# A depthwise convolution inside an attention kernel: from whole 128-token chunks with half of the TensorE array per head to half chunks with a quarter of the array per head, added up from two PSUM banks

## The chip, the cores and the metric

The kernel runs on one core of one Trainium2 chip. The metric is device time in microseconds for one execution of the whole program; the median of three runs is used.

## The reference

There are two layers on a feature map of 2 batches, 512 channels and 64 x 32 = 2048 tokens. All numbers are fp32.

Layer 0 is a full softmax attention with 8 heads of 64 channels. Layer 1 is a Nystrom attention: with 256 landmarks per head it forms three softmax matrices, takes a pseudo-inverse of the middle one in 6 iterations, and adds to the attention's result a convolution of the values along the tokens:

```python
attn2_pinv = moore_penrose_iter_pinv(attn2, PINV_ITERS)
out = attn1 @ (attn2_pinv @ (attn3 @ v))
pad = KERNEL // 2
res = lax.conv_general_dilated(v, conv_w, window_strides=(1, 1), padding=((pad, pad), (0, 0)),
                               dimension_numbers=('NCHW', 'OIHW', 'NCHW'), feature_group_count=h)
out = out + res
```

`KERNEL` is 33. Every head has one filter of 33 taps, which runs over the head's 2048 tokens in each of its 64 channels. An output projection, a normalisation and a linear map (4-bit weights times a second matrix) follow. The change concerns only `res`.

## The kernel before

The kernel works on **pairs of heads**: 2 batches x 4 pairs make 8 pairs, and 2 heads x 64 channels fill the 128 partitions. Layer 0 takes the first part of the program (up to about 1620 us), then come the projections of layer 1 for all pairs, and from about 1800 us on the pairs of layer 1 are worked through one after the other in the order of `todo` (batch 1 first, then batch 0). The main loop (`for n, pair in enumerate(todo)`) runs `pair.pinv(chunk, last)`. The pseudo-inverse of pair n is a chain of dependent matmuls, and between its steps the callbacks `chunk` and `last` put work of the neighbouring pairs: `attn1` of pair n-1 (`before`), `attn3`, the convolution and the landmarks of pair n+1 (`after`), the value projection of pair n+2, and at n >= 4 the output stage of batch 1 (`finish`).

The order of the instructions of PE, DVE, ACT and POOL is the order in which the code writes them (`tc.manual_schedule(engines=in_order)`). The queue of SP, which starts most DMAs, is ordered by the scheduler.

The **convolution** of pair n+1 stands in `chunk(NTB)`, after the last full iteration of the pseudo-inverse: `landmarks = after.landmarks_values(); next(landmarks); drain(convolution(n + 1))`. Only the first pair is different: `second_of_first` puts its convolution in two parts among the projections (1728.5 and 1738.8 us). The convolution is done as a matmul with a band matrix. `write_bands` writes for every head a row with the 33 taps into DRAM in such a way that, read back with a row length that is one shorter, each partition's copy is shifted by one; `prefetch` loads the band of a pair (tile `band`, one buffer). `convolution` (line 1433 is its matmul) goes over 4 blocks t of 512 tokens. For each it takes one PSUM bank `cv`, lets every chunk of 128 tokens that reaches into the block add 160 columns (128 plus 16 on either side) in each head's half of the bank's partitions, and ACT copies the bank out (line 1442, or 1445 followed by a DMA to `o_fd`). The chunks overlap by 32 columns, so the matmuls of a block accumulate.

Four further facts are needed to follow the steps:

- PSUM in this part has four banks in one pool (tag `pp`), two for products of the pseudo-inverse and two side banks. `bank(...)` takes one of the four, which go round in the order in which they come free; `cv`, the row sums `rs` of `landmarks_values` (line 1380), the transposes `tp_M` of `flip` (line 1496) and `wp` of `product_transposed` (line 1481) all come from the four.
- Ahead of the convolution `chunk(NTB)` writes the end of the last `attn1` block of pair n-1: `attn1_inverse` (line 1595, DVE reciprocal) and `attn1_end` (line 1600, DVE product, then POOL adds into `o`). At n = 5 and 6 a step of `finish` is next (lines 957, 958 and 962, DVE). Then `landmarks_values` writes an ACT copy (line 1389), a DVE reciprocal (line 1390) and a DVE product (line 1391). All of these stand ahead of the convolution in the queue of DVE.
- After the convolution `pinv` goes on with `flip` for both heads (PE transposes `tp_M`, ACT copies M, line 1497), and with `product_transposed`, whose second half of matmuls needs the flipped M. Then comes the value projection `vp` (line 924) of pair n+2.
- For `todo[5]` and `todo[6]` `o` is None: the rows go through a two-buffer tile (`row_of`, tag `rinv`) and by DMA to `o_fd`, so the third row waits for the first row's DMA. The last pair has a buffer of its own again.

Of the kernel before, what the change touches and what calls it, by code (L numbers as in the profile page):

```python
# [10 lines left out]
F32 = mybir.dt.float32  # L11
I32 = mybir.dt.int32
AF = mybir.ActivationFunctionType
ALU = mybir.AluOpType
AX = mybir.AxisListType

P = 128
# [3 lines left out]
HEADS, D = 8, 64  # L21
NPAIR = HEADS // 2
TB = 512
NTB = S // TB
NST = S // P
LM, POOL = 256, S // 256
PINV_ITERS = 6
KER, HALO = 33, 16
# [624 lines left out]

CUBE = 0.25 ** (1.0 / 3.0)

BAND = P + 2 * HALO

GAP = object()

# [2 lines left out]
def fast_path(  # L662
# [35 lines left out]
    nc = tc.nc  # L698
    dram = ctx.enter_context(tc.tile_pool(name="dram1", bufs=1, space=bass.MemoryType.DRAM))
# [20 lines left out]
    o_d = dram.tile([B, NPAIR, P, S], F32, name="o_fd")  # L720
    A_d = dram.tile([B, NPAIR, 2, P, 2, LM], F32, name="A_fd")
    L_d = dram.tile([B, NPAIR, P, 2, LM], F32, name="L_fd")
    band_d = dram.tile([HEADS, P * (BAND + 1)], F32, name="band_fd")

    def chunked(ap):
        return ap.rearrange("(k p) n -> p k n", p=P)
# [1 line left out]
    def bank(name):  # L728
        return ps.tile([P, 512], F32, tag="pp", name=name)
# [21 lines left out]
    def block_of(pool, tag, name):  # L751
        return pool.tile([P, KC, TB], F32, tag=tag, name=name)

    def row_of(name):
        return apool.tile([P, TB], F32, tag="rinv", name=name)
# [417 lines left out]
    def write_bands():  # L1173


        rows = block_of(lpool, "xn", "rows1").rearrange("p k n -> p (k n)")
        rows = rows[:, : HEADS * (BAND + 1)].rearrange("p (h q) -> p h q", h=HEADS)
        nc.vector.memset(rows, 0.0)
        nc.sync.dma_start(rows[:, :, :KER], convr.partition_broadcast(P))
        for h in range(HEADS):  # L1180
            nc.sync.dma_start(band_d[h].rearrange("(p q) -> p q", q=BAND + 1), rows[:, h, :])

    class Pair:
# [120 lines left out]
        def prefetch(self):  # L1304
            self.k = kvpool.tile([P, S], F32, tag="v", name=f"k2_{self.name}")
            nc.sync.dma_start(self.k, k_d[self.b, self.hp])
            self.L = [lmpool.tile([P, LM], F32, tag="L0", name=f"L0_2_{self.name}")]
            nc.sync.dma_start(self.L[0], L_d[self.b, self.hp][:, 0, :])
            self.band = lmpool.tile([P, 2, BAND], F32, tag="band", name=f"band_{self.name}", bufs=1)
            for h in range(2):  # L1310
                src = band_d[2 * self.hp + h][: P * BAND].rearrange("(p q) -> p q", q=BAND)
                nc.sync.dma_start(self.band[:, h, :], src)

        def values(self, xhs):
            v = kvpool.tile([P, NST, P], F32, tag="v", name=f"v_{self.name}")
# [104 lines left out]

        def convolution(self, o):

            self.o = o
            for t in range(NTB):
                toks = slice(t * TB, (t + 1) * TB)
                cv = bank(f"cv_{self.name}_{t}")
                near = [c for c in range(4 * t - 1, 4 * t + 5) if 0 <= c < NST]
                for c in near:
                    at = c * P - HALO - t * TB
                    lo, hi = max(0, -at), min(BAND, TB - at)  # L1430
                    for h in range(2):
                        half = slice(h * D, (h + 1) * D)
                        nc.tensor.matmul(  # L1433
                            cv[half, at + lo : at + hi],
                            lhsT=self.v[:, c, half],
                            rhs=self.band[:, h, lo:hi],
                            start=c == near[0],
                            stop=c == near[-1],
                            skip_group_check=True,
                        )  # L1440
                if o is not None:
                    nc.scalar.copy(o[:, toks], cv)
                else:
                    row = row_of(f"o_{self.name}_{t}")
                    nc.scalar.copy(row, cv)
                    nc.sync.dma_start(o_d[self.b, self.hp][:, toks], row)
                if t % 2:
                    yield

# [228 lines left out]
    for n, (b, hp) in enumerate(todo[:-1]):  # L1678
        nb, nhp = todo[n + 1]
        if nb != b:  # L1680
            xbs = load_x(x, nb, "x0")
        nxt = Heads0(nb, nhp, xbs)
        n_fill = Heads0.N_UNITS + 2 * len(work)
        if finish is None:
            units = nxt.units(wait=nb - b)
        else:

            units = nxt.units(False, lambda: outs_done)
            work.append(finish)
            n_fill += N_FINISH0  # L1690
        work.append(units)
        attention0(cur, work, n_fill, units, ffn_map if finish is None else None, finish is not None)
        finish = None
        oTs.append(cur.q)
        if n == 3:
            while ffn_map:
                advance(ffn_map)
            wo_sb = load_wo(wo0, "wo_f0")
            write_bands()
        if hp == NPAIR - 1:  # L1700
            outs_done = []
            finish = finish0_units(b, oTs, outs_done)
            oTs = []
        cur = nxt
# [126 lines left out]
    def second_of_first():  # L1831
        pair = todo[0]
        yield from values(0)
        yield from pair.attn3()
        landmarks, start, conv = pair.landmarks_values(), pair.start_values(), convolution(0)
        for part in (landmarks, conv, landmarks, start, conv):
            next(part)
            yield
        drain(conv)
        next(start)  # L1840
        yield
# [26 lines left out]
    for n, pair in enumerate(todo):  # L1868
# [16 lines left out]
        if n:  # L1885
            q = late_buffer if n > NPAIR + 1 else lambda name: kvpool.tile([P, S], F32, tag="k", name=name)
            pair.prefetch1(q(f"q2_{pair.name}"))

        def chunk(c):
# [5 lines left out]
            if c == NTB:  # L1895
                if after:
                    landmarks = after.landmarks_values()
                    next(landmarks)
                    drain(convolution(n + 1))
                else:  # L1900
                    advance(finish, 2)
                return
# [126 lines left out]
@with_exitstack  # L2029
def conv_attn_hybrid(  # L2030
    ctx: ExitStack,
    tc: tile.TileContext,
    x: bass.AP,
    emb: bass.AP,
    freq: bass.AP,
    time: bass.AP,
    wq0: bass.AP,
    wk0: bass.AP,
    wv0: bass.AP,
    wo0: bass.AP,  # L2040
    b0: bass.AP,
    *rest: bass.AP,
):

    nc = tc.nc
    keep = ctx.enter_context(tc.tile_pool(name="keep_f", bufs=1))
    bad = keep.tile([P, 1], F32, name="bad")
    bad_i = keep.tile([P, 1], I32, name="bad_i")
    in_order = {mybir.EngineType.PE, mybir.EngineType.DVE, mybir.EngineType.Activation, mybir.EngineType.Pool}
    with tc.manual_schedule(engines=in_order):  # L2050
        fast_path(tc, x, freq, time, wq0, wk0, wv0, wo0, b0, *rest, bad)
    nc.vector.tensor_copy(bad_i, bad)
    again = nc.values_load(bad_i[:1, :1])
    with tc.If(again > 0):
        general_path(tc, x, emb, wq0, wk0, wv0, wo0, b0, *rest)
# [59 lines left out]
```

## Time and profile before

| | |
|---|---|
| median of 3 runs | 2808.86 us (2808.78 to 2810.7) |
| profiled execution, its own time | 2808.29 us |
| profiled execution, span from first to last instruction | 2806.2 us |
| granted TensorE clock, mean | 0.993 |
| busy: PE / PE weight loads / DVE / ACT / POOL | 98% / 49% / 63% / 33% / 8% |
| convolution on PE (line 1433) | 704 matmuls, 40.3 us |

A line of the groups names the line of code, the engine, the operation and the tiles, then the busy time in us and the mean ns of one instruction, then the idle time just before and what ended it. In "128*64 128x160" the first part is the piece of the array that is used (rows*columns), the second the moving operand. One fp32 matmul of the code appears as two MATMUL records with a weight load (LDWEIGHTS) each, called passes below: 352 matmuls of the convolution are 704 records. Matmuls of several pieces of the array that stand next to each other run side by side, so the busy time divided by the count is smaller than the duration of one.

### The profile page before, as it was taken

Reading aid. Unit: us, or ns where it says so; the run is one execution under the profiler, and the core shown is the slowest. Engines: PE = TensorE matmul, PEld = TensorE weight load, DVE = VectorE, ACT = ScalarE, POOL = GpSimd, SP = SyncE. Lnnn points to the kernel's source line nnn. Section 1 sums busy time; section 2 is a strip of 40 time slices with the busy share of each in tenths; the row PEclk is TensorE's granted clock in tenths of the full one; section 3 lists DMA queues with packets and bytes.
Section 4 is the critical chain, followed back from the end, with each engine's and each line's share of the span. In section 5 each row is a group of like instructions: output and inputs, shape, how many; then the busy total and the mean of one; then the engine's idle time right before and its main releaser. Section 6 shows DMA issues by size and latency. Waiting matters only on the chain. (4 is left out here: it accounts for less than half of the span.)

```text
span 2806.2 us, 39647 instructions
## 1 busy us (share of the span) xinstructions
PE 2745.0 (98%) x16746; PEld 1374.3 (49%) x16746; DVE 1778.3 (63%) x2109; ACT 913.5 (33%) x1352; POOL 231.7 (8%) x130
## 2 busy tenths in 40 slices
PE   9999999999999999999999999999999999999899
PEld 5343443434343334343344455777667666554333
DVE  2868788784658775767767544545755655556565
ACT  1434343433334334434422223223332323222110
POOL 1101101010101210100002000000100100000000
PEclk9999999999999999999999999999999999999999
DMA  3000000101001200002025632203001102010201
GB/s 113 5 5 1 5 1 1 61 16 46 27 32 60 75 1 1 1 31 67 16 83 180 202 120 89 97 28 114 27 28 50 65 1 86 23 61 19 101 16 46
DMA packets 85626, 140.31 MB, mean 50 GB/s; under 512 B 7856, under 2 KB 42944, under 8 KB 82880
## 3 DMA queue, kind: packets, MB, share of 16 engines
q1 hardware_dynamic: 80944, 120.87, 12.8%
q0 software_dynamic: 4416, 16.79, 1.6%
q8 instruction: 133, 2.18, 0.3%
q14 instruction: 53, 0.43, 0.0%
q10 hardware_dynamic: 80, 0.03, 0.0%
HBM read 82.48 MB, written 55.19 MB: 49 GB/s over the span
## 5 line engine op out<-in xcount | busy, mean ns | idle before, releaser
L1058 DVE TENSOR_TENSOR acc_f<-acc_f,p_f 128x1024 f32<-128x1024 f32 x448 | 611.4, 1365 | 217.8 <-ACT p_f L1048 188.8
L1048 ACT ACTIVATE p_f<-sc_f 128x1024 f32<-128x1024 f32 x512 | 496.8, 1022 | 580.2 <-PE sc_f L1040 574.1
L1040 PE MATMUL sc_f<-q_f,k_f 64*64 64x512 f32 x4096 | 491.7, 595 | 2.9 <-ACT p_f L1048 2.9
L1070 PE MATMUL av_f<-p_f,v_f 64*64 64x512 f32 x4096 | 484.3, 589 | 0.0
L1070 PEld LDWEIGHTS av_f<-p_f,v_f 64*64 64x64 f32 x4096 | 156.5, 133 | 283.0 <-issue 283.0
L1040 PEld LDWEIGHTS sc_f<-q_f,k_f 64*64 64x64 f32 x4096 | 144.8, 133 | 293.8 <-issue 253.0
L1214 PE MATMUL pp<-xh,w 128*128 128x512 f32 x512 | 231.2, 604 | 4.6 <-ACT X L1261 3.9
L1214 PEld LDWEIGHTS pp<-xh,w 128*128 128x128 f32 x512 | 95.7, 192 | 125.8 <-issue 113.9
L1506 PE MATMUL pb<-R 128*128 128x192 f32 (+1 forms) x640 | 149.6, 380 | 1.0 <-DVE M L1519 1.0
L1506 PE MATMUL pa<-M 128*128 128x192 f32 (+1 forms) x640 | 150.6, 380 | 0.0
L1595 DVE RECIPROCAL acc<-acc 128x256 f32<-128x256 f32 x64 | 111.4, 1746 | 46.7 <-ACT acc L1590 46.7
L1089 POOL TENSOR_TENSOR q_f<-q_f,rinv_f 128x512 f32<-128x512 f32 x32 | 68.3, 2135 | 825.6 <-DVE rinv_f L1088 825.5
L1601 POOL TENSOR_TENSOR o<-o,acc 128x512 f32<-128x512 f32 x32 | 53.8, 1682 | 885.1 <-DVE acc L1600 778.1
L924 PE MATMUL vp<-w,xh 128*128 128x128 f32 x1024 | 122.3, 278 | 0.0
L924 PEld LDWEIGHTS vp<-w,xh 128*128 128x128 f32 x1024 | 118.6, 194 | 7.2 <-issue 4.2
L924 PEld LDWEIGHTS vp_f<-wv_f,x 128*128 128x128 f32 x1024 | 115.6, 192 | 12.7 <-issue 11.0
L879 PE MATMUL pp_q_f<-x,wq_f 128*128 128x512 f32 x256 | 117.5, 612 | 4.2 <-DVE q_f L882 3.1
L939 PE MATMUL yp_f<-q_f,wo_f 128*128 128x512 f32 x256 | 115.9, 606 | 4.2 <-DVE rinv_f L1088 3.3
L924 PE MATMUL vp_f<-wv_f,x 128*128 128x128 f32 x1024 | 118.5, 276 | 0.0
L1506 PEld LDWEIGHTS pb<-R 128*128 128x128 f32 x640 | 106.5, 190 | 24.4 <-DVE M L1519 2.1
L1506 PEld LDWEIGHTS pa<-M 128*128 128x128 f32 x640 | 108.2, 193 | 20.4 <-ACT M L1497 2.5
L1654 PE MATMUL fp_g<-xn_g,mT 128*128 128x512 f32 x256 | 115.1, 598 | 0.7 <-ACT p L1568 0.7
(202 smaller groups left out, 3009.6 us busy)
## 6 DMA issues: line engine op xcount, KB each, us to landing
xh<-xh_fd SPq DMA_DIRECT2D x12, 1024.0 KB, 5.4
xr_f<-in_x_dram SPq DMA_DIRECT2D x8, 1024.0 KB, 5.1
x_fd<-xr_f POOLq DMA_DIRECT2D x8, 1024.0 KB, 4.7
xh_fd<-xn_f POOLq DMA_DIRECT2D x8, 1024.0 KB, 4.6
k_fd<-k SPq DMA_DIRECT2D x32, 256.0 KB, 2.7
q_fd<-q SPq DMA_DIRECT2D x32, 256.0 KB, 3.0
xb_g<-x_fd SPq DMA_DIRECT2D x32, 256.0 KB, 4.5
k<-k_fd SPq DMA_DIRECT2D x8, 1024.0 KB, 5.9
```

Source lines behind the costliest of these rows:

```text
L879: nc.tensor.matmul(pp, lhsT=w_sb[kind][:, k, cols], rhs=xbs[t][:, k, :], start=k == 0, stop=k == KC - 1)
L924: nc.tensor.matmul(vp[:, j * P : (j + 1) * P], lhsT=xb[:, k, j * P : (j + 1) * P], rhs=w_of(k), start=k == 0, stop=k == KC - 1,)
L939: nc.tensor.matmul(yp, lhsT=wo_sb[:, k, m * P : (m + 1) * P], rhs=oTs[k][:, toks], start=k == 0, stop=k == NPAIR - 1,)
L1040: nc.tensor.matmul(sc[r * D : (r + 1) * D, h, :], lhsT=hd.k[rows, lo : lo + D], rhs=hd.q[rows, t * TB : (t + 1) * TB], start=True, stop=True,)
L1048: nc.scalar.activation(p, sc, AF.Exp, scale=D**-0.5)
L1058: nc.vector.tensor_tensor(acc, first if c == 1 else acc, p, ALU.add)
L1070: nc.tensor.matmul(av[r][half, :], lhsT=hd.v[keys, c, half], rhs=pp[keys, h, :], start=c == 0, stop=c == NST - 1,)
L1089: nc.gpsimd.tensor_tensor(o, o, rinv, ALU.mult)
L1214: nc.tensor.matmul(pp, lhsT=self.w[j][:, c, :], rhs=xhs[t][:, c, :], start=c == 0, stop=c == KC - 1)
L1506: nc.tensor.matmul(dst, lhsT=lhsT[:, k, t * P : (t + 1) * P], rhs=rhs[:, k, :], start=k == 0, stop=k == 1)
L1595: nc.vector.reciprocal(half, half)
L1654: nc.tensor.matmul(fp, lhsT=mT[:, k, m * P : (m + 1) * P], rhs=self.xn[:, k, :], start=k == 0, stop=k == KC - 1,)
```

## The change

The 128-token chunk is split into two halves of 64 tokens (r = 0, 1), which are the lower and the upper 64 partitions of `v`. A half chunk reaches 16 tokens further on either side, 96 columns in all; the band row is laid out so that each matmul writes 128 columns, the 96 and 32 in which the band is zero. Even halves write columns that lie side by side without overlap or gap, and so do odd halves. The even ones go to one bank, the odd ones to another (`cvs[0]`, `cvs[1]`), each matmul with `start=True, stop=True`. A head's half chunk uses 64 rows and 64 columns of the array. ACT copies one bank to the destination, and DVE adds the other bank onto it in place; at the ends of the sequence, where one of the banks isn't filled in full, it is the one that is added, with 480 columns. The band is loaded into both halves of the partitions, with four DMAs in place of two.

```diff
-BAND = P + 2 * HALO
+BAND = P
...
-    band_d = dram.tile([HEADS, P * (BAND + 1)], F32, name="band_fd")
+    band_d = dram.tile([HEADS, D * (BAND + 1)], F32, name="band_fd")
...
-        rows = rows[:, : HEADS * (BAND + 1)].rearrange("p (h q) -> p h q", h=HEADS)
+        rows = rows[:D, : HEADS * (BAND + 1)].rearrange("p (h q) -> p h q", h=HEADS)
         nc.vector.memset(rows, 0.0)
-        nc.sync.dma_start(rows[:, :, :KER], convr.partition_broadcast(P))
+        nc.sync.dma_start(rows[:, :, HALO : HALO + KER], convr.partition_broadcast(D))
...
-                src = band_d[2 * self.hp + h][: P * BAND].rearrange("(p q) -> p q", q=BAND)
-                nc.sync.dma_start(self.band[:, h, :], src)
+                src = band_d[2 * self.hp + h][: D * BAND].rearrange("(p q) -> p q", q=BAND)
+                for r in range(2):
+                    nc.sync.dma_start(self.band[r * D : (r + 1) * D, h, :], src)
...
-                cv = bank(f"cv_{self.name}_{t}")
-                near = [c for c in range(4 * t - 1, 4 * t + 5) if 0 <= c < NST]
-                for c in near:
-                    at = c * P - HALO - t * TB
-                    lo, hi = max(0, -at), min(BAND, TB - at)
-                    for h in range(2):
-                        half = slice(h * D, (h + 1) * D)
-                        nc.tensor.matmul(
-                            cv[half, at + lo : at + hi],
-                            lhsT=self.v[:, c, half],
-                            rhs=self.band[:, h, lo:hi],
-                            start=c == near[0],
-                            stop=c == near[-1],
-                            skip_group_check=True,
-                        )
-                if o is not None:
-                    nc.scalar.copy(o[:, toks], cv)
-                else:
-                    row = row_of(f"o_{self.name}_{t}")
-                    nc.scalar.copy(row, cv)
-                    nc.sync.dma_start(o_d[self.b, self.hp][:, toks], row)
+                cvs = [bank(f"cv{r}_{self.name}_{t}") for r in range(2)]
+                for c in range(max(4 * t - 1, 0), min(4 * t + 5, NST)):
+                    for r in range(2):
+                        at = c * P + r * D - 2 * HALO - t * TB
+                        lo, hi = max(0, -at), min(BAND, TB - at)
+                        if lo >= hi:
+                            continue
+                        rows = slice(r * D, (r + 1) * D)
+                        for h in range(2):
+                            half = slice(h * D, (h + 1) * D)
+                            nc.tensor.matmul(
+                                cvs[r][half, at + lo : at + hi],
+                                lhsT=self.v[rows, c, half],
+                                rhs=self.band[rows, h, lo:hi],
+                                start=True,
+                                stop=True,
+                            )
+                dst = o[:, toks] if o is not None else row_of(f"o_{self.name}_{t}")
+
+                full, part, cols = cvs[0], cvs[1], slice(2 * HALO if t == 0 else 0, TB)
+                if t == NTB - 1:
+                    full, part, cols = cvs[1], cvs[0], slice(0, TB - 2 * HALO)
+                nc.scalar.copy(dst, full)
+                nc.vector.tensor_tensor(dst[:, cols], part[:, cols], dst[:, cols], ALU.add)
+                if o is None:
+                    nc.sync.dma_start(o_d[self.b, self.hp][:, toks], dst)
```

## Prediction

> **What bounds the kernel now.** I read the page's shares of the span, then the groups, then the timeline of one convolution, engine by engine. The page and its groups:
>
> ```profile
> PE 2745.0 (98%) x16746; PEld 1374.3 (49%) x16746; DVE 1778.3 (63%) x2109; ACT 913.5 (33%) x1352; POOL 231.7 (8%) x130
> ...
> L1433 PE MATMUL cv<-band,v 128*64 128x144 f32 (+2 forms) x704 | 40.3, 270 | 0.0
> L1077 DVE TENSOR_TENSOR q_f<-av_f,q_f 128x512 f32<-128x512 f32 x32 | 22.0, 689 | 8.0 <-ACT q_f L1076 8.0
> L1442 ACT COPY o<-cv 128x512 f32<-128x512 f32 x24 | 14.1, 587 | 16.4 <-PE cv L1433 16.4
> ```
>
> PE is busy 98% of the span and the convolution's matmuls never wait (idle 0.0), so every us that the convolution takes or waits on PE is a us of the program, unless PE waits for the same thing later anyway. ACT waits for PE, not PE for ACT. The other two lines are prices. Now one of the seven convolutions in the main loop (the one that starts at 2030.28), first DVE's timeline, then PE's (start, length, engine, line):
>
> ```profile
> 2030.14 1.75 DVE L1595 RECIPROCAL acc<-acc 128x256 f32<-128x256 f32 x1
> 2031.93 0.69 DVE L1600 TENSOR_TENSOR acc<-av,acc 128x512 f32<-128x512 f32 x1
> 2032.54 1.74 DVE L1390 RECIPROCAL acc<-acc 128x256 f32<-128x256 f32 x1
> 2034.38 0.42 DVE L1391 TENSOR_TENSOR acc<-av,acc 128x256 f32<-128x256 f32 x1
> 2040.98 0.48 DVE L1519 SCALAR_TENSOR_TENSOR R<-M,tp 128x128 f32<-128x128 f32 x2 [6.17 <-PE tp L1490]
> ```
>
> ```profile
> 2030.28 5.00 PE L1433 MATMUL cv<-band,v 128*64 128x144 f32 x88
> 2035.22 0.44 PE L1496 MATMUL tp_M<-ident,M 128*128 128x128 f32 x2
> 2035.58 1.37 PE L1481 MATMUL wp<-M 128*64 128x256 f32 x8
> 2036.88 3.84 PE L924 MATMUL vp<-w,xh 128*128 128x128 f32 x32
> ```
>
> DVE's share of 63% hides what matters: at just this place DVE has a queue of four instructions that ends at 2034.80, 4.52 us after the convolution began and 0.4 us before PE leaves it. Today nothing of the convolution is behind them. From here all times are counted from a convolution's first matmul: PE reaches tp_M at 4.93, wp at 5.30, vp at 6.60.
>
> [...]the trace has four copies of 587 ns per convolution whatever PE does. [...]at 1003.00, from 64*64 to 128*128, the trace shows a gap of 0.09 us. [...]above, DVE runs its four in the written order. [...]the eight 16-column matmuls from 1729.62 on start 25.4 ns apart on average, the densest 64 of the trace 50.8 ns.
>
> **The change part by part.**
>
> *PE, the passes.* From the single records: two 160-column matmuls side by side take 136 ns per pass, 144 columns 122 ns, 16 columns 59 ns[...]. So 128 columns take about 109 ns. In layer 0 four 64*64 matmuls of 512 columns start 7 ns apart and take 429 ns per pass, with their weight loads side by side, so I let four quarters of 128 columns take 109 ns as well. A block t becomes 4 steps of 128 columns and one at the seam, 2 passes each: 8 x 109 + 2 x 59 = 0.99 us. Today blocks follow each other after 1.27 us (the ACT copies start at 2031.61, 2032.87, 2034.14). Four blocks: 3.96 against 4.93 us, **0.97 less per convolution**, 7.8 us in eight, if nothing waits. Matmul records go from 704 to 1216 (76 matmuls per pair in place of 44). One more change of mode per convolution, 0.1 us, stays in the rounding.
>
> *DVE, the adds.* 32 instructions like line 1077, 0.69 us for 512 columns and 0.65 for 480, starting 0.6 us apart when they follow each other (the pace at which neighbours start above): 22 us on an engine with spare time. But in DVE's order they stand behind line 1391. If f is the time when 1391 ends, add 0 ends at f+0.58 and add 1 at f+1.20 (each starts up to 0.07 early).
>
> *Banks.* A block takes two of the four, and one of them is freed by the add. In the built program's order and waits, six of the seven loop convolutions have it so: block 2 needs the ACT copies of 0 and 1; **block 3 waits for add 0 and then add 1**; tp_M of head 1 waits for add 2; wp waits for the ACT copy of block 3. Queued behind the waiting matmul is all of PE. At n = 0 it is block 2 that waits for add 0, and block 3 for add 1.
>
> *Where PE comes out.* With f = 4.52: block 3 starts in earnest at f+1.26 = 5.78 and PE is through 0.87 later; ACT sees it 0.17 later and copies for 0.59; wp starts 0.06 after (7.47) in place of 5.30. Its first half takes 0.55, by which time both flips are in (today PE waits for them), its second 0.57: vp at 8.6 in place of 6.60, **2.0 later** (f+4.07). Three convolutions are of this kind (1931.5, 2030.3, 2129.1): 6.0 us. The others:
> - 1832.7 (no attn1 ahead): f = 2.93, block 2 starts at 3.57, block 3 ends at 5.45, vp at 7.4: +0.8.
> - 2227.8 (rows to DRAM): the third ACT copy waits for the first row's DMA, which now leaves after add 0. Today it lands 2.30 after the row is written (1.91 to 4.21). Row 0 at 5.10, copies of blocks 2 and 3 at 7.4 and 8.0, add 2 done at 8.74, then tp_M, flip, second half of wp: vp at 10.07 in place of 7.03: +3.0.
> - 2340.8 (rows, and lines 957/958 ahead): f = 7.34, row 0 at 7.92, by the same steps vp at 12.9 in place of 7.10: +5.8.
> - 2479.5 (line 962 ahead): f = 5.86, copy of block 3 done at 8.75, the next tp at 10.4 in place of 7.13: +3.3.
> - 1728.5 and 1738.8, the two parts of the first pair: PE has 3.4 us of projections after each, which cover the adds. 2 x 0.45 won: -0.9. Without this cover it would be as above, +2.
>
> Sum: -0.9 + 0.8 + 6.0 + 3.0 + 5.8 + 3.3 = **+18.0 us**. Later PE waits don't absorb it: the one for line 974 after 2340.8 begins with PE's own matmul at 10.77 and shifts too.
>
> *What costs nothing.* Two more SP issues per pair (0.42 us each) and a band that starts loading when PE leaves the convolution, later than today: behind it is the 1 MB load of k, 5.9 us to land, which is first read some 25 us later. The smaller memset and band rows lie in layer 0 beside PE. POOL's adds into o come a whole pair later. Cover gone, the k load would delay PE by at most 3 us per pair; I see no such place.
>
> **Rivals.**
> 1. *The adds wait for nothing that PE needs (faster).* If DVE reached add 1 by the time PE asks for block 3, at about 3.0, that is with f below 1.8, the passes' saving stands: 2808.9 - 7.8 = 2801. Against it: f is 2.93 to 7.34 in the seven loop convolutions. For it: only that the waits are from one execution.
> 2. *Quarters don't run at 109 ns per four.* 38 records per block break even at 1267/38 = 33 ns each. [...] If the two row halves took turns (1.9 us per block), block 3 would end 1 us later: about +26. The densest 64 matmuls at 50.8 ns don't rule out either; the 25.4 ns of eight speaks against the first, layer 0's four-wide passes against the second.
> 3. *Half the waits.* If ACT and DVE overlap better than in my steps (row DMAs earlier, flips ready), half of the 25.8 us of waiting is left: +5, 2814.
>
> That the change doesn't do what it says is excluded for order and banks, which the built program shows; rival 2 holds the rest.
>
> **How the numbers follow.** The profiled execution took 2808.29 us, 0.57 under the median of the runs, so the sum is put on the median: 2808.86 + 18.0 = 2826.9; I say 2826. Within 0.2% (5.6 us) a measurement of this kernel can't be told from no change. Chances: the forecast with its spread 0.71, rival 2 0.14, rival 3 0.10 (half of it within 0.2%), rival 1 0.05. So faster 0.05, the same 0.05, slower 0.90. The range from 2814 to 2843 leaves out rival 1 and the far end of rival 2.
>
> **What would show it.** In the profile after: matmuls of the convolution still with about 1 us per block, but a PE wait of 2 to 3 us before block 3 put down to DVE's add; the first add right behind line 1391; ACT copies at 2227.8 and 2340.8 waiting for o_fd longer than today's 1 us; vp about 2 us later after the three plain ones. Wrong if PE has no wait for the add, if the matmul starts within a block are over 33 ns apart on average, or if line 1391 ends later or earlier than f here.

## The result, and the profile after

The changed kernel takes **2837.01 us** (median of 4 runs, 2836.24 to 2838.53) where the kernel before takes 2808.82 beside it (2808.51 to 2810.7): ratio **1.0103**, 95% interval 1.0088 to 1.0118. Measured again later it took 2834.79 against 2807.87, ratio 1.0098 (1.0083 to 1.0114). It is 27 to 28 us slower; the forecast was 18 us slower. The profiled execution took 2836.47 us, its span is 2834.7 us and its mean granted clock 0.986 (0.993 before).

The shares of the span say next to nothing (PE 97% in place of 98%, DVE 63% as before). The groups of the convolution's tile `cv` say what it is made of (count, then ns: least, median, most). There are 1216 matmul records in place of 704, and 32 adds:

```profile
L1438 PE MATMUL cv<-band,v x1216: 189/269/473, 1731.0 to 2510.4; 64*64 64x128 f32 x111, 64*64 64x96 f32 x37, 64*64 64x32 f32 x26
L1450 ACT COPY o<-cv x32: 586/586/587, 1732.2 to 2510.8; 128x512 f32<-128x512 f32 x32
L1451 DVE TENSOR_TENSOR o<-cv,o x32: 647/669/692, 1735.4 to 2511.4; 128x480 f32<-128x480 f32 x16, 128x512 f32<-128x512 f32 x16
```

The matmuls of the convolution never waited before. Among PE's waits between 1720 and 2600 us (us in total, times, longest) they now stand twice, behind DVE's add and behind ACT's copy; of these lines only the one for 974 was there in the kernel before:

```profile
PE cv L1438 <- DVE o L1451: 13.1, 13, 4.0
PE var_g L974 <- DVE sq_g L971: 9.5, 3, 4.4
PE cv L1438 <- ACT o L1450: 3.8, 6, 0.7
...
PE tp_M L1503 <- ACT o L1450: 1.6, 2, 1.2
...
PE tp_M L1503 <- DVE o L1451: 0.9, 3, 0.4
```

The plain convolution shown before now starts at 2035.93. DVE's timeline first, then PE's (start, length, engine, line; in brackets the wait and who ended it):

```profile
2038.08 1.74 DVE L1391 RECIPROCAL acc<-acc 128x256 f32<-128x256 f32 x1
2039.93 0.42 DVE L1392 TENSOR_TENSOR acc<-av,acc 128x256 f32<-128x256 f32 x1
2040.27 1.84 DVE L1451 TENSOR_TENSOR o<-cv,o 128x480 f32<-128x480 f32 x3
```

```profile
2035.93 2.12 PE L1438 MATMUL cv<-band,v 64*64 64x96 f32 x80
2038.68 1.12 PE L1438 MATMUL cv<-band,v 64*64 64x96 f32 x36 [0.63 <-ACT o L1450]
2040.97 0.30 PE L1438 MATMUL cv<-band,v 64*64 64x32 f32 x4 [1.17 <-DVE o L1451]
2041.57 1.05 PE L1438 MATMUL cv<-band,v 64*64 64x96 f32 x32 [0.29 <-DVE o L1451]
2042.55 0.44 PE L1503 MATMUL tp_M<-ident,M 128*128 128x128 f32 x2
2043.33 1.08 PE L1488 MATMUL wp<-M 128*64 128x256 f32 x8 [0.34 <-ACT o L1450]
2044.34 0.82 PE L924 MATMUL vp<-w,xh 128*128 128x128 f32 x5
```

Blocks 0 and 1 fill the four banks in about 2.1 us. ACT copies one bank of each at once, but three adds come in a row only at 2040.27, directly behind the product that was line 1391 and is now 1392: the other two banks stayed full as long as DVE was busy with other work. PE waits for a copy near the beginning of block 2 (0.63 us) and for the adds in block 3 (1.17 us before its first four records and 0.29 us after them), and vp starts 8.41 us after the convolution's first matmul (6.60 before).

### The profile page after: what moved, and what is told of

It is laid out like the page before. It is cut to its first block, busy times and chain, and to the rows that moved or that the text cites. A ratio compares the mean times of both kernels' runs of the same rounds, so it can differ in the third digit from the quotient of the medians.

```text
span 2834.7 us, 40694 instructions
## 1 busy us (share of the span) xinstructions
PE 2753.3 (97%) x17258; PEld 1374.7 (48%) x17258; DVE 1798.4 (63%) x2141; ACT 913.5 (32%) x1352; POOL 233.2 (8%) x130
```

## The experiments

Times are set against the kernel before, run on the same chip in the same group (2808.35 us for the first four, 2807.87 for the next four, 2808.06 and 2807.67 for the two last pairs). A warning for comparing single profiles: everything before the first convolution is the same code, and yet it ended between 4.4 us earlier and 2.5 us later than in the profile of before. Where profiles are compared below, it is by how much more the same PE instructions lag (or lead) behind each convolution than ahead of it. A second thing to know: the clock record of a profile consists of stretches in which a share of 1.0 is granted and stretches in which it is 0.5 (in the kernel before 9 of the latter, in the changed kernel 16). One of the latter is called a run of half clock below.

### No adds

```diff
-                nc.vector.tensor_tensor(dst[:, cols], part[:, cols], dst[:, cols], ALU.add)
```

> Changed kernel without DVE's 32 adds: the second bank of each block is computed and never read, so the odd halves are missing from the convolution's result. Theory: what is left is the shorter passes, four blocks of 0.94 us with at most 0.2 us of waiting, that is about 1.0 us less than before in each of eight convolutions: 2801 us (2799 to 2804). Rival A (matmuls dear): 2815 or more.

**2800.39 us**, ratio 0.9973 (0.9963 to 0.9983). The passes alone do what was forecast of them. PE's timeline of a plain convolution has no wait in it:

```profile
2025.16 3.86 PE L1438 MATMUL cv<-band,v 64*64 64x96 f32 x152
...
2030.66 1.60 PE L924 MATMUL vp<-w,xh 128*128 128x128 f32 x12
```

The 152 records take 3.86 us (5.00 before for 88), 25 ns each on average, and vp starts at 5.50 in place of 6.60. The four quarters do run side by side here (from 2036.10 us on in the changed kernel, four records of 128 columns start every 109 ns, where one of them lasts 269); rival 2 of the prediction is out.

### All of DVE's other work behind the convolution

```diff
             rinv = self.acc3[:, 0, :]
             nc.scalar.copy(rinv[:, :LM], rs[:, :LM])
+            between()
             nc.vector.reciprocal(rinv[:, :LM], rinv[:, :LM])
```

`between` writes the convolution, then the end of `attn1` and the step of `finish`, which are taken away ahead of it.

> Changed kernel, with the end of attn1, the step of finish and the landmarks' reciprocal and product written after the convolution instead of before it, so that nothing of theirs is ahead of the adds on DVE; matmuls, banks and instructions are the same in number. Theory (the adds stand behind DVE's queue and hold the banks): the ACT copy and the add follow each block at once, PE waits about 0.6 us before block 2 and not at all or under 0.3 us before block 3, vp starts 6.4 to 6.6 us after the first matmul as in the kernel before (6.60), no run of half clock follows the convolutions, and the time is 2807 us (2803 to 2811). Rival A (quarter matmuls or their changes of mode are dear in themselves): the order matters little, 2830 or more. Rival B (the 32 adds as such load DVE and delay its later work): part of the loss stays, 2815 to 2825.

**2812.48 us**, ratio 1.0015 (1.0008 to 1.0022). 23 of the 27 us are gone with the order alone, which is the theory's main point; but the expected 2803 to 2811 us were missed. A plain convolution on PE:

```profile
2026.56 2.12 PE L1439 MATMUL cv<-band,v 64*64 64x96 f32 x80
2029.07 2.02 PE L1439 MATMUL cv<-band,v 64*64 64x96 f32 x72 [0.39 <-DVE o L1452]
...
2032.92 1.27 PE L924 MATMUL vp<-w,xh 128*128 128x128 f32 x9
```

vp starts at 6.36, as expected. Up to 2335 us the profile holds its lead; it loses 4.2 us right behind the convolution near 2340 and 3.7 at the last. DVE's line 958 near 2340 shows one reason, first in the kernel before (where the convolution starts at 2340.82), then here (2337.93):

```profile
2344.32 1.65 DVE L958 TENSOR_TENSOR xn_g<-xn_g 128x512 f32<-128x512 f32 x1
```

```profile
2348.34 1.64 DVE L958 TENSOR_TENSOR xn_g<-xn_g 128x512 f32<-128x512 f32 x1
...
2352.01 2.28 DVE L962 TENSOR_TENSOR xn_g<-xb_g,mean_g 128x2048 f32<-128x2048 f32 x1
```

Line 958 ends 12.0 us after the convolution's first matmul where it ended at 5.2 before. PE's line 961 reads its result and begins at 12.1 (10.8 before), and line 962 ends at 16.4 (14.1 before). So DVE's later work is held back, as rival B has it, at these two convolutions, where `finish` shares DVE, and at none of the others. But the load of the adds is the smaller part: the end of `attn1`, now behind them, begins 6.9 us later than before, of which the four adds are 2.7 us of work; for the rest DVE stands waiting for the copies ahead of its adds.

The other reason is the half clock, which the expectation had excluded. The profile has 20.0 us of it between 1720 and 2560 us (6.8 in the kernel before). In the run of half clock from 2352.22 on, the 32 matmuls of vp take 5.14 us in place of 3.74:

```profile
2352.70 5.14 PE L924 MATMUL vp<-w,xh 128*128 128x128 f32 x32
```

A longer one, 10.24 us, begins at 2488.76, inside a wait of 4.5 us for line 1393 at the last convolution. How the loss divides between the two reasons was not tested.

### Only the landmarks' work behind the convolution

```diff
-                    landmarks = after.landmarks_values()
-                    next(landmarks)
-                    drain(convolution(n + 1))
+                    landmarks = after.landmarks_values(lambda: drain(convolution(n + 1)))
+                    next(landmarks)
```

> Changed kernel, with only the landmarks' reciprocal and product (2.16 us of DVE) written after the convolution; the end of attn1 and the step of finish stay ahead of it. Theory of the queue: the adds come 2.16 us earlier than in the changed kernel, f is about 2.4 instead of 4.5 in the plain convolutions, 5.1 instead of 7.2 in the one that starts at 2356 and 3.7 instead of 5.9 in the last; vp about 7.0 after the first matmul in the plain ones (8.4 before this edit, 6.6 in the kernel before); the sum over the convolutions is about +6.6 us, with one or two runs of half clock 2817 us (2812 to 2823). Rival A (matmuls dear): 2830 or more. Rival B (adds as load): like the first run, 2815 to 2825, with no difference between the two.

**2813.84 us**, ratio 1.0019 (1.0011 to 1.0026), inside the range. One plain convolution:

```profile
2030.15 2.12 PE L1439 MATMUL cv<-band,v 64*64 64x96 f32 x80
2033.01 1.99 PE L1439 MATMUL cv<-band,v 64*64 64x96 f32 x72 [0.74 <-DVE o L1452]
...
2036.86 1.38 PE L924 MATMUL vp<-w,xh 128*128 128x128 f32 x10
```

With 2.16 us less ahead of the adds, PE waits for them 0.74 us, and vp starts at 6.70 (8.41 in the changed kernel, 6.36 in the run above); in the convolution near 2340 it starts at 11.56 in place of 13.74. Over all convolutions the profile loses 6.7 us against the kernel before (expected 6.6). The wait follows the length of DVE's queue. The times of this run and the one above can't be told apart (2811.84 to 2815.43 us and 2808.08 to 2815.12): in the profiles, moving the rest too gains 0.1 us at each plain convolution and loses 0.8 at the last two together.

### Matmuls in the waits

```diff
+                for cols in fill.get(t, []):
+                    nc.tensor.matmul(
+                        pr[:, :cols], lhsT=self.v[:, 0, :], rhs=self.v.rearrange("p c n -> p (c n)")[:, :cols],
+                        start=True, stop=True,
+                    )
                 cvs = [bank(f"cv{r}_{self.name}_{t}") for r in range(2)]
```

> Changed kernel, with idle-time matmuls of v by v on the whole array into a product bank that nobody reads, written where PE waits in the convolutions: they take 0.65 us before block 2 and 1.2 us before block 3 in the plain ones (waits there 0.85 and 1.39), 1.3, 5.0 and 2.9 us in all at 1834, 2356 and 2502, 0.95 after the one at 2238; always less than the wait. Everything else waits as long as before. Theory (about 10 us of the 28 are half clock that follows the waits): the clock stays at 1.0 through the convolutions and the time falls to 2829 us (2826 to 2832). Rival (the waits themselves were underestimated, the clock is a detail): nothing is gained, 2837 to 2840.

**2824.79 us**, ratio 1.0063 (1.005 to 1.0077): with more matmuls than the changed kernel, it is 10 us faster than it (control below), more than was expected. Near 2340 it lost again: between the DMAs of the first two rows lay 3 us on SP, the last ACT copy came at 12.39 and vp at 14.98 (13.74 in the changed kernel).

> As the run with filler matmuls, but before block 3 of the convolution with rows to DRAM that starts at 2356 only 3.0 us of them instead of 3.9, and none behind that convolution. Theory: the time of the run before without what that convolution lost there, 2823 us (2820 to 2826), the forecast's sum at full clock. Rival (filler only displaces): equal to the changed kernel.

**2825.36 us**, ratio 1.0074 (1.006 to 1.0088). It is within the range, but not faster than the longer filler. In the profiles it loses less, 17.0 us against the kernel before from 1700 to 2500 us, where the longer filler loses 20.5; but the longer filler's profile is 3.8 us further ahead at 1700 us, in code that no edit touches. And the control, in the same group:

> The changed kernel once more, unaltered, beside the others of this group and with more rounds, because in the profiles the projections and layer 0, which no edit touches, end between 4.4 us earlier and 2.5 us later than in the profile of the kernel before, with the runs of half clock that fall there. Theory (that part is chance, not the change): the time stays 8 to 12 us over the next run with filler matmuls, and the half clock after the convolutions is there again, 20 us or more of it between 1720 and 2560 beyond that of the kernel before. Rival (the first measurement was high by chance in the early part): 2829 to 2833 us, 4 to 6 us over the filler's.

**2834.79 us**: 9.4 us over the shorter filler by the medians. The size is less certain than the sign: two of the filler's five runs took 2831 us, at a mean clock of 0.991 in place of 0.993, and even these are under all four of the control. PE's timeline of a plain convolution with filler, at which nothing has become earlier (vp at 8.41, as without it):

```profile
2033.28 0.91 PE L1430 MATMUL fill<-v 128*128 128x384 f32 x2
...
2035.20 1.45 PE L1430 MATMUL fill<-v 128*128 128x512 f32 x4
...
2039.70 1.05 PE L924 MATMUL vp<-w,xh 128*128 128x128 f32 x7
```

What has changed is the clock. Stretches of 10 us from about the beginning of two convolutions, first in the changed kernel, then with the shorter filler (length, then busy time and count of PE, PEld, DVE, ACT, POOL, then **PE's clock**, DMA share, GB/s):

```profile
2137.00:2147.00 10.00, 7.84 (x162) 5.84 (x155) 6.32 (x8) 3.19 (x8) 1.27 (x1) 0.83 0.05 12
...
2502.00:2512.00 10.00, 6.77 (x158) 5.48 (x160) 7.84 (x9) 3.06 (x7) 1.27 (x1) 0.80 0.02 3
2512.00:2522.00 10.00, 6.93 (x28) 3.12 (x26) 4.05 (x7) 4.92 (x8) 0.00 (x0) 0.52 0.14 39
```

```profile
2132.00:2142.00 10.00, 9.63 (x184) 7.34 (x183) 6.67 (x8) 3.43 (x8) 1.28 (x1) 1.00 0.05 12
...
2492.60:2502.60 10.00, 9.52 (x172) 6.14 (x170) 8.08 (x9) 3.13 (x8) 1.28 (x1) 1.00 0.01 2
2502.60:2512.60 10.00, 6.61 (x25) 3.08 (x26) 5.73 (x6) 5.27 (x9) 0.00 (x0) 0.83 0.14 39
```

Between 1720 and 2560 us the clock record has 37.5 us at half clock in the changed kernel and 34.1 in its repetition, but 6.8 with the shorter filler, as many as in the kernel before. So the **half clock** that follows PE's waits costs 9 to 10 us of the 27 by the medians.

### Looking for a better place: two halves around the first projection

```diff
+                conv.append(convolution(n + 1))
+                next(conv[0])
...
+            if i == 0 and after:
+                drain(conv[0])
```

> The changed convolution in two halves, as the first pair has it: blocks 0 and 1 ahead of the end of attn1, of finish and of the landmarks' reciprocal and product in DVE's order, blocks 2 and 3 behind the first value projection that follows (3.8 us of PE). Theory of cover: each half finds its four banks free, the adds run beside PE's projection, PE waits at most 0.5 us per convolution, and of the shorter passes' 1.0 us per convolution most is kept: 2803 us (2800 to 2807), faster than the kernel before. Rival (the adds hold back the landmarks' transpose or the steps of finish at 2228 to 2480, as they did in the first run): 2808 to 2813.

**2808.63 us**, ratio 1.0005 (0.9996 to 1.0013): the rival's number. On PE, in a plain pair:

```profile
2030.80 0.33 PE L1504 MATMUL tp_M<-ident,M 128*128 128x128 f32 x1 [0.18 <-DVE o L1452]
...
2037.90 0.44 PE L1498 MATMUL tp<-ident,R 128*128 128x128 f32 x2
2038.48 0.44 PE L1401 MATMUL tp<-ident,acc 128*128 128x128 f32 x2
```

The second flip waits for a bank that an add holds, and the two transposes behind blocks 2 and 3 start 0.58 us apart where it was 0.22 before. A plain pair gains 0.15 us, but the convolution near 2340 loses 2.0 and the last one 2.8. The kernel before in that order:

> The kernel before with the same order of two halves and its own 160-column matmuls and single bank per block: tells what of the previous run's time comes from the order alone. Theory: PE had no wait in the convolution, so the order wins nothing by itself, 2808 us (2806 to 2811), and the quarters' gain in that order is 4 to 6 us. Rival (the order alone makes the gain, as the flips' waits go): 2803 to 2805.

**2808.67 us**, ratio 1.0001 (0.9992 to 1.0009). The order wins nothing, as expected; that the quarters win 4 to 6 us in it is refuted.

### Ahead of the projections

```diff
-                    drain(convolution(n + 1))
+                    conv.append(convolution(n + 1))
...
+            if i < 2 and after:
+                next(conv[0])
```

> The changed convolution in two halves, now each directly ahead of a value projection of the main loop (blocks 0 and 1 behind the first wp and ahead of the first vp, blocks 2 and 3 behind the landmarks' transpose and ahead of the second vp), with DVE's order of the rest left as in the changed kernel. Theory of cover: the projection needs one bank at its start and takes 3.8 us, so both adds of a half run beside it although they stand behind DVE's queue; what is left is about 0.3 us of waiting for banks ahead of block 2 (for ACT's copy of the projection) and 0.3 us for the flips, so some 0.4 to 0.6 us per convolution are won, and the time is 2805 us (2802 to 2808). Rival (wherever it stands, the pair's chain between PE, ACT and DVE gives the passes' gain back, as in the run with two halves around the first projection): 2808 to 2812.

**2806.09 us**, ratio 0.9997 (0.9989 to 1.0005): within the range, but the interval includes no change at all. A plain pair gains 0.6 us, the convolution at 2228 1.0, the last 2.6, and the one near 2340 loses 4.2 right behind it. There PE waits for line 974 for 6.4 us in one piece:

```profile
PE var_g L974 <- DVE sq_g L971: 10.8, 2, 6.4
```

The kernel before in that order:

> The kernel before, its own matmuls and single banks, with its convolution in the same two places ahead of the projections. Theory: the order alone wins nothing, since PE did not wait in the convolution, and the flips lose the cover that the convolution gave them: 2809 us (2807 to 2812), 3 to 6 us more than the quarters in that order. Rival (the gain of the previous run is one of order): within 1 us of it.

**2804.31 us**, ratio 0.9986 (0.998 to 0.9993): my expectation failed. The order alone wins time, and by the medians it wins 1.8 us more with the old matmuls than with the quarters (the two intervals overlap). Its waits for the same line, behind those of the kernel before in its own order:

```profile
PE var_g L974 <- DVE sq_g L971: 9.9, 3, 4.4
```

```profile
PE var_g L974 <- DVE sq_g L971: 6.9, 2, 4.4
```

The profile puts the gain at the last convolution (3.5 us; 0.1 us lost at each plain one): one of the three waits for line 974, of 3.0 us, is gone, and the convolution's matmuls are what PE does instead. The run of half clock that began behind that wait is gone too, and a wait of 1.5 us for line 1391 is new.

### Ahead of the projections, but not where rows and `finish` meet

```diff
+                    if n == NPAIR + 1:
+                        next(conv[0])
...
+            if i == 0 and n == NPAIR + 1:
+                drain(conv[0])
```

> The changed convolution ahead of the projections as in the run of that name, except for the one with rows to DRAM that starts near 2340: its blocks 0 and 1 stay in their old place behind DVE's queue, its blocks 2 and 3 follow directly behind the first projection, ahead of line 961. In the run ahead of projections this convolution lost 4.2 us against the kernel before, because its last rows left so late that line 968 waited for their buffers and line 974 for 968, while the plain ones won 0.6 each, the one at 2228 1.0 and the last 2.6. Theory: flips and wp take the two banks that ACT frees, adds 0 and 1 run beside the projection, rows 2 and 3 leave 4 us earlier, and this convolution comes out even (within 1 us): 2802 us (2800 to 2805), faster than the kernel before. Rival (adds 2 and 3 push line 962 back, or the banks do): 2805 to 2808.

**2803.38 us** (21 runs), ratio **0.9985** (0.9979 to 0.9992). The convolution near 2340 costs 1.0 us right behind it and 0.6 by the next one, as expected. The kernel before in that order:

> The kernel before, its own matmuls and single banks, in the order of the previous run. Theory: as the kernel before ahead of projections, 2804 us (2802 to 2806), of which 3.5 us come at the last convolution and none at the plain ones; the quarters win the difference to the previous run, about 2 us. Rival (the quarters win nothing in any order): equal to the previous run or faster.

**2803.47 us** (21 runs), ratio 0.9985 (0.9979 to 0.9992). The rival holds: both versions are 4 us faster than the kernel before, and the medians show no difference between quarters and old matmuls. In the two profiles they win 0.7 us at each plain pair and give it back at the last two convolutions, where the kernel before's matmuls win 3.8 us against 0.3; at the last one the quarters' profile has a run of half clock that the other lacks. (From 1700 us on the quarters' profile is ahead by 2.4 us, but it is of the fastest of its 21 runs; I don't count that.)

## Why the prediction was right, and what it missed

The growth of the lag against the profile of before, from ahead of one convolution to ahead of the next (for the last, to 2500 us), in us:

| convolution (start before) | forecast | changed | changed, again | shorter filler |
|---|---|---|---|---|
| first pair, two parts | -0.9 | -1.3 | -1.3 | -1.3 |
| 1832.7 | +0.8 | +0.8 | +0.8 | +0.9 |
| 1931.5 | +2.0 | +3.5 | +1.9 | +1.9 |
| 2030.3 | +2.0 | +1.9 | +3.2 | +1.9 |
| 2129.1 | +2.0 | +3.1 | +1.9 | +1.9 |
| 2227.8, rows | +3.0 | +4.6 | +6.0 | +2.9 |
| 2340.8, rows and `finish` | +5.8 | +7.1 | +5.7 | +5.3 |
| 2479.5 | +3.3 | +5.3 | +5.7 | +3.3 |
| sum | +18.0 | +25.0 | +23.9 | +17.0 |

The sums are those of the unrounded steps. What the changed kernel has over the sums comes before 1700 us and after 2500 us, 0 to 2.5 us each.

- **The passes.** Forecast 0.99 us per block, measured 0.94 (the ACT copies of blocks 0 and 1 start 0.94 apart). Right, and the first pair wins more for it. Without adds a convolution is 1.1 us shorter, forecast 0.97.
- **The adds behind DVE's queue.** Right to 0.2 us: line 1391 (now 1392) ended at 4.42 (forecast f = 4.52), the first add began at 4.34, block 3 got its second bank at 5.64 (forecast 5.78), vp began at 8.41 (8.6). One sign in the prediction was off: it looked for a wait of 2 to 3 us before block 3, and there were 1.5. PE came to block 3 later than it says, at 3.87, because it had waited 0.63 us at block 2 for ACT's copy; as block 3 has to wait for the adds anyway, the end stays the same.
- **Rows.** Right. Near 2340 f was 7.23 (forecast 7.34), the first row's DMA was issued at 7.83, and ACT's third copy began at 10.07, after standing idle for it; vp began at 13.74, and at 13.02 with the shorter filler (forecast 12.9):

```profile
2366.16 1.18 ACT L1450 COPY o<-cv 128x512 f32<-128x512 f32 x2 [7.37 <-DMA o_fd<-o]
```

- **The step that failed: the sum was made at full clock.** The prediction took PE's passes after a wait at their usual durations (in the changed kernel the 32 records that end block 3 took 1.05 us at full clock from 2041.57 on, and 1.88 us from 2364.54 on, in a run of half clock). The filler, which keeps DVE's adds and vp at the plain convolutions where they were, brings the sum to 17.0 and each step to within 0.5 us of the forecast's; the half clock adds 7 to 8 us to the sum over the convolutions, and 9.4 us to the median. The mechanism and the sign of the prediction stand; this term was set at nothing, without a reason. That the spread around the forecast covers it all the same is luck: it was made wide for rival 2, not for the clock. The profile of before held the hint: two of its runs of half clock, 3.41 us each from 2362.0 and 2491.7, begin 1.0 and 1.4 us after a wait for line 974 ended.
- **Rivals.** 1 is excluded by the 13.1 us of waits for the add, 2 by the run without adds (25 ns per record, under the 33 ns at which the prediction has them break even; its far end was an estimate that no run of this case shows), 3 by the table. That *what costs nothing* holds for the band and the k load is not refuted: neither appears among PE's waits.

Left open: what the quarters would win where no PSUM bank is short. The run without adds, 8 us under the kernel before, is the bound that the shorter passes set here; no run gave the convolution more of them.

## What to carry to other kernels

In this kernel the accumulation that was taken off TensorE and given to DVE took DVE's queue into TensorE's path (13.1 us of waits for the adds): count what stands ahead of the add, and how many banks there are until it has run. Here a wait on TensorE cost its own length and often some of the clock behind it (37.5 us of half clock between 1720 and 2560 us, 6.8 before), so where a profile shows such runs, price a schedule's waits also by how they sum up within the length of one, 3.41 us here. If the order must change to make an edit pay, run the old code in the new order too; here the order was the whole gain.

## What the runs showed of the hardware that I had not expected

In the clock records all runs of half clock begin on a grid of 3.413 us that runs through the whole execution (9 runs in the profile of before and 16 in the changed kernel's, each within 0.001 us of it), and last a multiple of it (3.41, 6.83, 10.24, 13.65), apart from the one that the end of the program cuts off (6.23 us before, 4.51 in the changed kernel). I laid that grid over the 14 profiles from 1720 to 2560 us and took for every cell the share of it in which PE has a matmul record:

| cell at full clock, PE busy | cells | next cell at half clock |
|---|---|---|
| under 0.5 | 36 | 33 |
| 0.5 to 0.6 | 19 | 6 |
| 0.6 to 0.7 | 26 | 1 |
| 0.7 and over | 3322 | 0 |

Of 57 cells at half clock, the 20 in which PE was busy for less than 0.95 were followed by another one, the 37 busier ones by full clock. In these profiles half clock did not come behind long pauses alone: in the changed kernel the cell from 1937.9 us on, in the convolution that starts at 1933.64, has 1.4 us of waiting in pieces (busy share 0.59) and is followed by 3.41 us of half clock. The convolution at 2035.93, with the same instructions and waits, lies otherwise on the grid, with two cells of 0.67 and 0.62, and has none. This goes with the way the column of the changed kernel in the table above jumps between 1.9 and 3.5, and changes place in its repetition.

Between 100 and 1720 us, most of it layer 0, the ends of the table are the same (under 0.5: 36 cells of 36; 0.7 and over: none of 6513), but not the middle: 1 of 10 cells with 0.5 to 0.6 and 10 of 41 with 0.6 to 0.7 are followed by half clock, and of 17 cells at half clock with PE busy for less than 0.95, 8. The busy share of a cell thus does not tell all of it; what else matters stays open.
